# The four stages of an edge network, one group apart or two: a graph-network kernel on one Trainium2 core

## The chip, the core and the metric

The kernel runs on one core of one Trainium2 (trn2) chip. The metric is the device time of one execution in microseconds, without compilation. The median of three runs of the kernel before is 21820.6 us (21802.45 to 21820.88); smaller is better.

Engines are named as in the profile: PE is TensorE's matmul unit and PEld its weight loading, DVE is VectorE, ACT is ScalarE, POOL is GpSimd, SP is SyncE, which here only issues DMAs.

## What is computed

A graph has 6250 nodes with 48 features and 200000 edges sorted by their end node. Four parts follow one another; after each one the result is added to the node features and layer-normed. The second part is the one that matters here:

```python
def _L1_gnn_ref(x, edge_index, edge_feat, W1, b1, W2, b2, W3, b3):
    source, target = edge_index
    edge = jnp.concatenate([x[source], x[target], edge_feat], axis=-1)   # 48 + 48 + 16 = 112
    h = jax.nn.relu(edge @ W1 + b1)                                       # 112 -> 128
    h = jax.nn.relu(h @ W2 + b2)                                          # 128 -> 128
    message = h @ W3 + b3                                                 # 128 -> 48
    msum = jax.ops.segment_sum(message, target, num_segments=n)
    cnt = jax.ops.segment_sum(ones, target, num_segments=n)
    return x + msum / jnp.maximum(cnt, 1.0)[:, None]
...
x = _layernorm(x + _L0_gnn_ref(...)); x = _layernorm(x + _L1_gnn_ref(...))
x = _layernorm(x + _L2_gnn_ref(...)); x = _layernorm(x + _L3_gnn_ref(...))
```

The first part is a four-layer attention over the same edges, the third and fourth are weighted sums of neighbours. All arithmetic of the second part is float32.

## The kernel before

The edges lie as 128 partitions by 1564 columns, so that one column is 128 edges, one in each partition. The columns are worked off in 41 chunks: 38 of 40 columns, then 24, 12 and 8 (`CHUNKS`). Everything is written with a framework that records instructions in program order, lets a scheduler place them on the engines' queues, and adds the semaphore waits. Each engine then works its queue off strictly in that order.

`edge_mlp` is the second part's edge network. For each chunk it does this:

- Two DMAs from SP load `r` (the edges' rows: end nodes, weight, 16 edge features; line 1190) and `q` (the target's features, which stand only in the first edge of each run of equal targets; line 1192).
- `segments_chunk` (lines 801 to 803, DVE) takes from `r` the index `other` of the source node and the mask `ns` of the runs. An ACT copy keeps the edge weight (line 1194).
- POOL gathers the source's features with one indirect DMA for each column (`gather`, line 167): 40 of them for a chunk, into `t[:, j, 0:H]`. The tile `t` has two buffers, so the gathers of chunk c+2 wait until chunk c's `t` has been read.
- `runs` (lines 268, 270 and 287) spreads `q` over each run: ACT copies a quarter of the features to PSUM, DVE adds the value carried from the chunk before and runs a scan over it. ACT then copies the result into `t` (line 1202) and the edge features too (line 1203).
- The network itself works in groups of 4 columns (512 edges), ten groups in a full chunk, in four stages:
  - `turn`: 4 PE transposes into `ps_t` (line 1209), ACT copies them to `at` (line 1211);
  - `first_layer`: one PE product into `ps_1` (line 1216), ACT applies bias and relu into `h1` (line 1218);
  - `second_layer`: one PE product into `ps_1` (line 1223), DVE applies bias and relu into `h2` (line 1225);
  - `third_layer`: 4 PE products into `ps_3` (line 1231), DVE copies them to `msg` (line 1232).
- `runs` sums `msg` over each run (the scans into `sf`), ACT copies the sums to `st` (line 1239) and issues the DMA that stores them.

`ps_t` and `ps_1` have two buffers each, `ps_3` has one; `at`, `h1` and `h2` have the pool's two; `q` has two as well. `skewed` sets the program order of the four stages: in step i the first stage works on group i, the second on group i-1, the third on i-2, the fourth on i-3. So a full chunk has 13 steps, and when the last group is transposed (step 9) the layers of its step and three more steps are left. In the trace a transpose shows as one PE matmul record, the products of lines 1216 and 1223 as two each (float32), the four products of line 1231 as eight, so a group makes 4 + 2 + 2 + 8 = 16 records.

After a chunk's last `msg` copy, ACT and DVE work through the sums of that chunk and the spreading of the next chunk's `q`; only then can the next chunk's transposes begin, since these read `t`, into which line 1202 writes.

Of the kernel before, what the change touches and what calls it, by code (L numbers as in the profile page):

```python
# [9 lines left out]
F32 = mybir.dt.float32  # L10
# [9 lines left out]
P = 128  # L20
N, E, H = 6250, 200000, 48
# [9 lines left out]
HID = 128  # L31
# [5 lines left out]
def pj(t):  # L37
    return t.rearrange("(p j) w -> p j w", j=J)
# [7 lines left out]
def gnn_kernel(ctx: ExitStack, tc: tile.TileContext, A, out: bass.AP):  # L46
# [119 lines left out]
    def gather(dst, table, idx):  # L166
        return nc.gpsimd.indirect_dma_start(  # L167
            out=dst, out_offset=None, in_=table, in_offset=bass.IndirectOffsetOnAxis(ap=idx, axis=0))
# [37 lines left out]
    def by_columns(pool, wid, w, name, cols=C, **kw):  # L206

        return pool.tile([P, cols, w], F32, name=name, **kw)[:, :wid, :]

    def by_features(pool, w, wid, name, cols=C, **kw):  # L210

        t = pool.tile([P, w, cols], F32, name=name, **kw)
        return t.rearrange("p f c -> p (f c)")[:, :w * wid].rearrange("p (f c) -> p f c", c=wid)
# [28 lines left out]
    def factors(pool, name, fg=FG, cols=C):  # L242

        ts = [pool.tile([P, fg, cols], F32, name=f"{name}{i}", bufs=1) for i in range(2)]
        for t in ts:
            V.memset(t, 0.0)

        def put(c, v):
            wid = v.shape[1]
            t = ts[c % 2].rearrange("p f c -> p (f c)")[:, :fg * wid]  # L250
            u = t.rearrange("p (f c) -> p f c", c=wid)
            if wid < cols:
                V.memset(u[:, :, 0:1], 0.0)
            S.copy(u[:, :, 1:], v[:, None, 1:].to_broadcast([P, fg, wid - 1]))
            return t
        return put

    def runs(psum, dst, fac, first, before_, w, put, fg=FG, cols=C):


        wid = dst.shape[2]
        flat = dst.rearrange("p f c -> p (f c)")
        for f0 in range(0, w, fg):
            n = min(fg, w - f0)
            v = by_features(psum, fg, wid, "run_v", cols)
            put(v[:, :n, :], f0, n)
            if before_ is not None:
                V.scalar_tensor_tensor(v[:, :n, 0], before_[:, f0:f0 + n], first, v[:, :n, 0],  # L268
                                       op0=OP.mult, op1=OP.add)
            V.tensor_tensor_scan(flat[:, f0 * wid:(f0 + n) * wid], fac[:, :n * wid],  # L270
                                 v.rearrange("p f c -> p (f c)")[:, :n * wid], 0.0, OP.mult, OP.add)

    def kept_last(pool, t, name):

        k = pool.tile([P, t.shape[1]], F32, name=name)
        V.tensor_copy(k, t[:, :, t.shape[2] - 1])  # L276
        return k
# [4 lines left out]
    def by_column(t):  # L282
        return t.rearrange("p f c -> p c f")

    def copied(src):

        return lambda v, f0, n: S.copy(v, by_feature(src[:, :, f0:f0 + n]))  # L287
# [503 lines left out]
    def segments_begin(k, pool):  # L791
        prev = pool.tile([P, 1], F32, name="seg_prev", bufs=1)
        V.memset(prev, -1.0)
        nc.sync.dma_start(prev[1:P, :], pj(rows[k][:])[0:P - 1, J - 1, 0:1])
        f = pool.tile([P, 1], F32, name="seg_first", bufs=1)
        nc.sync.dma_start(f, pj(rows[k][:])[:, 0, 0:1])
        V.tensor_copy(seg0, f)
        return prev, f

    def segments_chunk(j0, wid, r, prev):  # L800
        V.tensor_copy(other[:, j0:j0 + wid], r[:, :, 1])
        V.tensor_tensor(ns[:, j0:j0 + 1], r[:, 0, 0:1], prev, op=OP.is_equal)
        V.tensor_tensor(ns[:, j0 + 1:j0 + wid], r[:, 1:, 0], r[:, 0:wid - 1, 0], op=OP.is_equal)
        return r[:, wid - 1, 0:1]
# [20 lines left out]
            T.transpose(ps, v.to_broadcast([P, P]), ident)  # L825
            V.tensor_copy(dst, ps)

    def skewed(n, *stages):

        kept = {}  # L830
        for i in range(n + len(stages) - 1):
            for k, stage in enumerate(stages):
                if 0 <= i - k < n:
                    kept[i - k] = stage(i - k, kept.get(i - k))

    carried = const.tile([P, H + 2], F32, name="carried")

# [42 lines left out]
    def first_rows(pool, table, name):  # L880
        t = pool.tile([P, H], F32, name=name, bufs=1)
        gather(t, table[:], seg0[:, 0:1])
        return t
# [6 lines left out]
    def gated_sums(ep, psum):  # L890
# [48 lines left out]
        for c, (c0, wid) in enumerate(CHUNKS):  # L939
# [29 lines left out]
            def outer(i, hi):  # L969
# [5 lines left out]
                V.tensor_mul(by_column(v)[:, j, 0:H], ps.rearrange("p k t w -> p (k t) w"), r[:, j, X0:X0 + H])  # L975

            skewed(-(-wid // 8), turn, hidden, outer)
            for _ in ahead:
                pass
# [201 lines left out]
    def edge_mlp(ep, psum, psum1, psum2):  # L1181
        W = 2 * H + EF
        prev, f = segments_begin("d", ep)
        factor = factors(ep, "fac")
        before_q = first_rows(ep, tab_x, "first")
        before_s = None
        for c, (c0, wid) in enumerate(CHUNKS):
            s = slice(c0, c0 + wid)
            r = by_columns(ep, wid, WD, "r")
            nc.sync.dma_start(r, pj(rows["d"][:])[:, s, :])  # L1190
            q = by_columns(ep, wid, H, "q")
            nc.sync.dma_start(q, pj(spread["d"][0:EP, :])[:, s, :])
            prev = segments_chunk(c0, wid, r, prev)
            S.copy(dw[:, s], r[:, :, 2])
            t = by_columns(ep, wid, W, "t")
            for j in range(wid):
                gather(t[:, j, 0:H], tab_x[:], other[:, c0 + j:c0 + j + 1])
            fac, first = factor(c, ns[:, s]), ns[:, c0:c0 + 1]
            qf = by_features(ep, H, wid, "qf", bufs=1)
            runs(psum2, qf, fac, first, before_q, H, copied(q))  # L1200
            before_q = kept_last(ep, qf, "last_q")
            S.copy(t[:, :, H:2 * H], by_column(qf))
            S.copy(t[:, :, 2 * H:], r[:, :, 3:])
            msg = by_columns(ep, wid, H, "msg", bufs=1)

            def turn(i, _):
                ps = psum.tile([W, 4, P], F32, name="ps_t")
                for k in range(4):
                    T.transpose(ps[:, k, :], t[:, 4 * i + k, :], ident)  # L1209
                at = ep.tile([W, 4, P], F32, name="at")  # L1210
                S.copy(at, ps)  # L1211
                return at

            def first_layer(i, at):
                ps = psum.tile([HID, 4, P], F32, name="ps_1")
                T.matmul(ps, w1, at, start=True, stop=True)  # L1216
                h1 = ep.tile([HID, 4, P], F32, name="h1")
                S.activation(h1, ps, AF.Relu, bias=b1)  # L1218
                return h1

            def second_layer(i, h1):
                ps = psum.tile([HID, 4, P], F32, name="ps_1")
                T.matmul(ps, w2, h1, start=True, stop=True)  # L1223
                h2 = ep.tile([HID, 4, P], F32, name="h2")
                V.tensor_scalar(h2, ps, b2, 0.0, op0=OP.add, op1=OP.max)  # L1225
                return h2

            def third_layer(i, h2):
                ps = psum1.tile([P, 4, H], F32, name="ps_3")
                for k in range(4):  # L1230
                    T.matmul(ps[:, k, :], h2[:, k, :], w3, start=True, stop=True)  # L1231
                V.tensor_copy(msg[:, 4 * i:4 * i + 4, :], ps)

            skewed(wid // 4, turn, first_layer, second_layer, third_layer)
            sf = by_features(ep, H, wid, "sf", bufs=1)
            runs(psum2, sf, fac, first, before_s, H, copied(msg))
            before_s = kept_last(ep, sf, "last_s")
            st = by_columns(ep, wid, H, "st", bufs=1)
            S.copy(st, by_column(sf))  # L1239
            nc.scalar.dma_start(pj(state_h[0:EP, :])[:, s, :], st)  # L1240
        lastf = ep.tile([P, 1], F32, name="lastf", bufs=1)
        V.tensor_copy(lastf, prev)
        return f, lastf, before_s

    with tc.tile_pool(name="e9", bufs=2) as ep:
        with tc.tile_pool(name="e9_ps", bufs=2, space=PSUM) as psum, \
                tc.tile_pool(name="e9_ps1", bufs=1, space=PSUM) as psum1, \
                tc.tile_pool(name="e9_ps2", bufs=2, space=PSUM) as psum2:
            f, lastf, sums = edge_mlp(ep, psum, psum1, psum2)
        with tc.tile_pool(name="e9_ps3", bufs=1, space=PSUM) as psum:  # L1250
            segments_end("d", ep, psum, f, lastf)
            carries(ep, psum, sums, H, 0)
# [112 lines left out]
```

## Time and profile before

| what | value |
|---|---|
| median of the runs | 21820.6 us |
| the profiled execution, its own time | 21803.16 us |
| its span, first to last instruction | 21801.4 us |
| mean granted TensorE clock | 0.621 |
| edge network (lines 1186 to 1240), first gather to last `msg` copy | 14098.9 to 17169.4 us |
| POOL busy over the span | 13861.4 us (64%) |
| PE busy over the span | 5648.7 us (26%) |
| DVE and ACT busy over the span | 8101.9 us (37%) and 4776.3 us (22%) |
| mean duration of one gather, `t<-tab_x` | 1020 ns |

Times are microseconds from the span's start unless marked ns. A timeline line gives start, duration, engine, line, operation, output and inputs, the shape and the count, and in brackets how long the engine had been idle before it and who ended that; "remote" there means that the releaser is not among the instructions the profile can name. A line of the waits gives who waited for whom, the total, the times and the longest wait.

### The profile page before, as it was taken

Reading aid. Unit: us, or ns where it says so; the run is one execution under the profiler, and the core shown is the slowest. Engines: PE = TensorE matmul, PEld = TensorE weight load, DVE = VectorE, ACT = ScalarE, POOL = GpSimd, SP = SyncE. Lnnn points to the kernel's source line nnn. Section 1 sums busy time; section 2 is a strip of 40 time slices with the busy share of each in tenths; the row PEclk is TensorE's granted clock in tenths of the full one; section 3 lists DMA queues with packets and bytes.
Section 4 is the critical chain, followed back from the end, with each engine's and each line's share of the span. In section 5 each row is a group of like instructions: output and inputs, shape, how many; then the busy total and the mean of one; then the engine's idle time right before and its main releaser. Section 6 shows DMA issues by size and latency. Waiting matters only on the chain.

```text
span 21801.4 us, 86436 instructions
## 1 busy us (share of the span) xinstructions
PE 5648.7 (26%) x19138; PEld 3381.8 (16%) x19138; DVE 8101.9 (37%) x16477; ACT 4776.3 (22%) x6603; POOL 13861.4 (64%) x13410
## 2 busy tenths in 40 slices
PE   2332337622222222222222222244544200000000
PEld 2332334410001000110001000133333100000000
DVE  6554557743343434333433343322222211110001
ACT  0332334411111111111111111133333200001111
POOL 2566651177776777677776777644444577777777
PEclk9999995555555555555555555566666655555555
DMA  5455444422222222232222222211111111111111
GB/s 156 160 168 135 163 165 180 168 79 86 85 88 65 88 85 88 65 88 85 88 82 70 86 88 86 59 41 43 43 45 44 34 36 34 36 36 36 36 36 36
DMA packets 873557, 1792.31 MB, mean 82 GB/s; under 512 B 365490, under 2 KB 546658, under 8 KB 868034
## 3 DMA queue, kind: packets, MB, share of 16 engines
q1 hardware_dynamic: 349038, 860.63, 12.1%
q0 software_dynamic: 427520, 547.67, 10.9%
q10 hardware_dynamic: 96468, 378.32, 4.6%
q8 instruction: 163, 2.67, 0.1%
q14 instruction: 368, 3.01, 0.0%
HBM read 1144.48 MB, written 641.17 MB: 82 GB/s over the span
## 4 chain that ended last, share of the span: by engine, by line
POOL 29%; issue 13%; PE 6%; another core or an unknown queue 4%; DVE 3%; ACT 2%; DMA 0%; ACTq 0%; POOLq 0%; DVEq 0%; SPq 0%
POOL t L167 28%; PE ps L1216 2%; PE ps L1223 2%; PE ps L1231 2%; POOL own L167 1%; PE ps_t L1209 1%; ACT run_v L287 1%; ACT st L1239 1%; DVE qf L270 1%; DVE sf L270 1%; DVE run_v L268 0%; DVE q L1134 0%; DMA t<-tab_x,other 0%; ACT at L1211 0%
## 5 line engine op out<-in xcount | busy, mean ns | idle before, releaser
L167 POOL DMA_INDIRECT t<-tab_kv,other x6256 | 6586.8, 1053 | 2117.7 <-issue 2075.2
L167 POOL DMA_INDIRECT t<-tab_x,other x4692 | 4787.2, 1020 | 2619.5 <-issue 1459.6
L1132 PE MATMUL ka<-t,ident 128*128 128x480 f32 (+2 forms) x1264 | 1209.1, 1060 | 6818.1 <-DMA t<-tab_kv,other 5869.4
L172 POOL DMA_INDIRECT rows_s<-r_s,scratch x1564 | 1524.8, 975 | 1032.8 <-ACT r_s L422 528.6
L1134 DVE TENSOR_TENSOR q<-qf,ka 128x480 f32<-128x480 f32 (+2 forms) x632 | 676.6, 1074 | 3791.7 <-issue 3146.9
L1132 PEld LDWEIGHTS ka<-t,ident 128*128 128x128 f32 x1264 | 316.8, 310 | 7533.7 <-issue 4066.5
L270 DVE TENSOR_TENSOR_SCAN qf<-fac,run_v 128x480 f32<-128x480 f32 (+1 forms) x943 | 1028.8, 1092 | 672.1 <-DVE run_v L268 357.1
L841 PE MATMUL cy_ps<-ident,last_s 128*48 128x128 f32 (+1 forms) x4 | 1.6, 405 | 4524.6 <-DVE last_s L276 4524.6
L1164 ACT COPY st<-m 128x40 f32<-128x40 f32 (+3 forms) x164 | 42.8, 261 | 4895.8 <-DVE sc L1137 3754.0
L387 PE MATMUL g<-hs,olt 128*128 128x49 f32 x3128 | 758.7, 417 | 1323.0 <-ACT hs L385 764.4
L287 ACT COPY run_v<-q 128x480 f32<-128x480 f32 (+1 forms) x943 | 851.8, 916 | 707.7 <-DMA q<-spread_s 258.6
L1133 PE MATMUL ka<-r,tenth 128*128 128x400 f32 (+2 forms) x1264 | 954.6, 858 | 0.0
L1225 DVE TENSOR_SCALAR h<-ps,b 128x512 f32<-128x512 f32 x391 | 293.6, 751 | 1710.6 <-PE ps L1216 902.9
L387 PEld LDWEIGHTS g<-hs,olt 128*128 128x128 f32 x3128 | 695.9, 327 | 1375.5 <-ACT hs L385 791.9
L1313 DVE TENSOR_TENSOR run_v<-t,w_ps 128x480 f32<-128x480 f32 (+3 forms) x164 | 142.1, 912 | 1832.9 <-DMA t<-tab_x,other 1832.9
L268 DVE SCALAR_TENSOR_TENSOR run_v<-last_s,ns,run_v 128x12 f32<-128x12 f32 x480 | 98.0, 219 | 1935.4 <-issue 1680.1
L924 POOL TENSOR_TENSOR r<-r,u 128x1920 f32<-128x1920 f32 (+3 forms) x41 | 135.5, 3305 | 1037.0 <-DVE u L923 958.7
L270 DVE TENSOR_TENSOR_SCAN sf<-dec,run_v 128x480 f32<-128x480 f32 (+5 forms) x820 | 731.3, 922 | 122.3 <-remote 57.1
L841 PEld LDWEIGHTS cy_ps<-ident,last_s 128*48 128x48 f32 (+1 forms) x4 | 0.5, 127 | 4525.3 <-ACT st L1319 2261.5
L1216 PE MATMUL ps<-at,w 112*128 112x512 f32 x782 | 535.7, 774 | 496.2 <-ACT h L1218 471.7
L1163 ACT COPY st<-sf 128x1960 f32<-128x1960 f32 (+3 forms) x164 | 621.1, 3787 | 44.9 <-DVE sf L270 25.1
L1156 DVE TENSOR_TENSOR run_v<-t,es 128x480 f32<-128x480 f32 (+2 forms) x656 | 616.7, 962 | 13.9 <-DVE sf L270 5.3
(395 smaller groups left out, 14775.8 us busy)
## 6 DMA issues: line engine op xcount, KB each, us to landing
q<-spread_s SPq DMA_DIRECT2D x190, 960.0 KB
state_a<-st ACTq DMA_DIRECT2D x152, 1000.0 KB
r<-rows_a SPq DMA_DIRECT2D x152, 820.0 KB
state_h<-st ACTq DMA_DIRECT2D x114, 960.0 KB
t<-tab_kv,other POOLq DMA_INDIRECT x6256
r<-rows_s SPq DMA_DIRECT2D x38, 2480.0 KB
t<-tab_x,other POOLq DMA_INDIRECT x4692
seed<-zeros SPq DMA_DIRECT2D x17, 3726.0 KB
```

Of the source, the lines that this page charges most:

```text
L167: return nc.gpsimd.indirect_dma_start(out=dst, out_offset=None, in_=table, in_offset=bass.IndirectOffsetOnAxis(ap=idx, axis=0))
L172: i = nc.gpsimd.indirect_dma_start(out=table, out_offset=bass.IndirectOffsetOnAxis(ap=idx, axis=0), in_=src, in_offset=None)
L270: V.tensor_tensor_scan(flat[:, f0 * wid:(f0 + n) * wid], fac[:, :n * wid], v.rearrange("p f c -> p (f c)")[:, :n * wid], 0.0, OP.mult, OP.add)
L287: return lambda v, f0, n: S.copy(v, by_feature(src[:, :, f0:f0 + n]))
L387: T.matmul(g[:, b0 + b, :], olt[:, b0 + b, :], hs[:, b, :], start=True, stop=True)
L1132: T.matmul(ka, ident, t[:, j0:j1, 0:H], start=True, stop=False)
L1133: T.matmul(ka[:, :, 0:RBF], tenth, r[:, j0:j1, 0:RBF], start=False, stop=True)
L1134: V.tensor_mul(q[:, j0:j1, :], by_column(qf)[:, j0:j1, :], ka)
L1156: V.tensor_mul(v, by_feature(t[:, :, H + 1 + f0:H + 1 + f0 + n]), es[:, None, :].to_broadcast([P, n, wid]))
L1163: S.copy(st[:, :, 0:H + 1], by_column(sf))
L1216: T.matmul(ps, w1, at, start=True, stop=True)
L1223: T.matmul(ps, w2, h1, start=True, stop=True)
```

## The change

The four stages of a group follow one another two groups apart: in step i the first stage works on group i, the second on i-2, the third on i-4, the fourth on i-6. A full chunk has 16 steps instead of 13. The tiles between the stages, `at`, `h1` and `h2`, get three buffers instead of two, and `q` gets one instead of two. No instruction is added or taken away, and the other users of `skewed` keep a distance of one.

```diff
-    def skewed(n, *stages):
+    def skewed(n, *stages, apart=1):
 
         kept = {}
-        for i in range(n + len(stages) - 1):
+        for i in range(n + apart * (len(stages) - 1)):
             for k, stage in enumerate(stages):
-                if 0 <= i - k < n:
-                    kept[i - k] = stage(i - k, kept.get(i - k))
+                g = i - apart * k
+                if 0 <= g < n:
+                    kept[g] = stage(g, kept.get(g))
...
-            q = by_columns(ep, wid, H, "q")
+            q = by_columns(ep, wid, H, "q", bufs=1)
...
-                at = ep.tile([W, 4, P], F32, name="at")
+                at = ep.tile([W, 4, P], F32, name="at", bufs=3)
...
-                h1 = ep.tile([HID, 4, P], F32, name="h1")
+                h1 = ep.tile([HID, 4, P], F32, name="h1", bufs=3)
...
-                h2 = ep.tile([HID, 4, P], F32, name="h2")
+                h2 = ep.tile([HID, 4, P], F32, name="h2", bufs=3)
...
-            skewed(wid // 4, turn, first_layer, second_layer, third_layer)
+            skewed(wid // 4, turn, first_layer, second_layer, third_layer, apart=2)
```

In the built program the order on PE, DVE and ACT differs only inside the edge network; POOL's order is the same, and SP issues the loads of `q` one chunk later.

## The prediction

> **What bounds the kernel now.** The busy shares first, for the even part of the edge network (14200 to 17000 us; the columns are the length, then busy time and count of PE, PEld, DVE, ACT and POOL, then the granted clock, the DMA share and GB/s). No engine is full. So I went on to the waits of the same stretch.
>
> ```profile
> 14200.00:17000.00 2800.00, 1385.54 (x5731) 882.45 (x5732) 793.37 (x1470) 1052.36 (x1185) 1358.99 (x1440) 0.69 0.15 43
> ```
> ```profile
> POOL t L167 <- ACT at L1211: 1006.0, 36, 30.5
> DVE h L1225 <- PE ps L1216: 900.0, 62, 27.7
> ...
> ACT at L1211 <- remote: 413.3, 60, 12.8
> ```
>
> POOL waits 28 us in every chunk until a chunk's last group is transposed and one buffer of `t` is free. ACT and DVE wait long for PE, once a chunk, and no instruction explains it. The timeline of one chunk shows where. I count from its first gather, 15003.71, and call what is left of the older chunk the tail and the next chunk's transposes and what runs beside them the head.
>
> ```profile
> 15002.35 0.61 PE L1209 MATMUL ps_t<-ident,t 128*112 128x128 f32 x4
> ...
> 15003.71 0.94 POOL L167 DMA_INDIRECT t<-tab_x,other  x1 [28.48 <-ACT at L1211]
> ...
> 15010.78 0.36 DVE L1232 COPY msg<-ps 128x192 f32<-128x192 f32 x1 [0.94 <-PE ps L1231]
> 15011.19 1.09 PE L1231 MATMUL ps<-w,h 128*128 128x48 f32 x8 [1.32 <-issue]
> 15015.73 0.36 DVE L1232 COPY msg<-ps 128x192 f32<-128x192 f32 x1 [4.59 <-remote]
> ...
> 15035.38 1.95 PE L1209 MATMUL ps_t<-ident,t 128*112 128x128 f32 x8 [23.09 <-issue]
> 15039.02 1.06 PE L1209 MATMUL ps_t<-ident,t 128*112 128x128 f32 x4
> 15048.82 0.58 ACT L1211 COPY at<-ps_t 112x512 f32<-112x512 f32 x1 [8.87 <-remote]
> 15052.40 0.94 POOL L167 DMA_INDIRECT t<-tab_x,other  x1 [0.30 <-issue]
> 15058.57 0.75 DVE L1225 TENSOR_SCALAR h<-ps,b 128x512 f32<-128x512 f32 x1 [26.95 <-PE ps L1216]
> 15080.55 0.61 PE L1209 MATMUL ps_t<-ident,t 128*112 128x128 f32 x4
> 15081.91 0.94 POOL L167 DMA_INDIRECT t<-tab_x,other  x1 [28.57 <-ACT at L1211]
> ```
>
> The last `msg` copy comes 2 to 4 us after PE shows its product done. Then come 19.65 us of scans (15015.73 to 15035.38). In the head, transposes shown as done at 15040.1 reach ACT only at 15048.82. The gathers end at 15053.3, and from 15058.57 on everything runs evenly to the last transpose. So one period is 49.6 us of gathers plus what is left of the head after them; from 14304.3 to 16943.8 us 34 periods take 77.6 us each.
>
> While POOL gathers, PE's results reach the others late. The price is plainest in the first chunk, which runs wholly beside gathers (they end at 14197.6):
>
> ```profile
> 14141.06 1.78 PE L1231 MATMUL ps<-w,h 128*128 128x48 f32 x8
> ...
> 14149.63 0.58 ACT L1211 COPY at<-ps_t 112x512 f32<-112x512 f32 x1 [16.17 <-remote]
> 14155.18 0.69 ACT L1218 ACTIVATE h<-ps,b 128x512 f32<-128x512 f32 x1 [4.96 <-remote]
> ...
> 14160.79 0.75 DVE L1225 TENSOR_SCALAR h<-ps,b 128x512 f32<-128x512 f32 x1 [21.66 <-remote]
> ...
> 14183.18 0.36 DVE L1232 COPY msg<-ps 128x192 f32<-128x192 f32 x1 [21.64 <-remote]
> ```
>
> These are deliveries in PE's order: 5.55 us for a first product (two records), 5.61 for a second (two), 22.39 for a third (eight). That is 2.8 us for each record, whatever its size. In the steady chunk the limit does not bite at once: of the 42 records that PE still has after a last transpose, 34 are delivered 7.1 us after the first gather and the last one at 12.0. Then PE rests 20 us, ten records of the head pass in time (ACT has the tenth at 15039.26), and the next four take 9.6 us. I read this as an allowance of some 42 records from the first gather on, refilled at one for each 2.8 us: 20 us give seven, and the head's first 4 us more than one, nearly the ten seen. What the mechanism is, the trace does not say. It is over about 4.4 us after the gathers, at +54.
>
> **The change, part by part.** *The order.* In a full chunk of 160 records, the last transpose (step 9) now stands after the first products of groups 0 to 6, the second of 0 to 4 and the third of 0 to 2: 40 + 14 + 10 + 24 = 88 records instead of 40 + 16 + 14 + 48 = 118. After it come 72 instead of 42. Thirty records move from before POOL's release to behind it.
>
> What this gains: the last transpose comes earlier. In the even stretch a step of 16 records takes 2.99 us, in which PE is busy throughout (2.00 of each 2.00 us from 15070 to 15082), so the larger distance makes no step shorter; DVE's 1.81 us waits there cost PE nothing. Thirty records fewer are 30/16 x 2.99 = 5.6 us.
>
> What it costs: the tail. Its first 42 records are delivered by +12, as now. The other 30 come beside gathers at 2.8 us. By +54 that is (54 - 12)/2.8 = 15; the remaining 15 (most of group 8's third product and all of group 9's) go at PE's own speed with the clock at half (1.78 us for eight), with two copies: about 4 us. The last `msg` copy is then at +58, where it is +12 now. Queued behind it in ACT's and DVE's order are this chunk's sums and the next chunk's spreading of `q`, and PE's next transposes wait for these: 19.65 us more, +77.6. The next head then meets no gathers at all. Such a head is in the trace once, behind the 24-column gather run:
>
> ```profile
> 17051.76 1.96 PE L1209 MATMUL ps_t<-ident,t 128*112 128x128 f32 x8 [21.70 <-issue]
> ...
> 17075.32 0.61 PE L1209 MATMUL ps_t<-ident,t 128*112 128x128 f32 x4
> ```
>
> From first to end of last transpose that is 24.2 us; less 5.6 it is 18.6. With 0.75 us to the next gather the period is 58 + 19.65 + 18.6 + 0.75 = 97 us, 19.4 more than now. It happens 36 times (chunks whose successor's successor has 40 columns): +698 us. Behind the 24-column gathers (29.6 us, now 55.3 from gather to gather) the same sum gives 29.6 + 4.4 + 4 + 19.65 + 18.6 + 0.75 = 77: +22. The three short chunks together I put at +10, the first chunk, which reaches its last transpose with fewer slow deliveries, at -10. Sum +720 us.
>
> The bounds: if the tail is through as soon as the limit ends (+54) and the head starts at full clock (its first eight transposes in 1.2 instead of 1.95 us), the period is 54 + 19.65 + 17.9 + 0.75 = 92 (+520 us in all, 22340). If nothing of the 5.6 us is gained in the head, because it begins cold and its first steps wait for ACT's copies, it is 58 + 19.65 + 24.2 + 0.75 = 103 (+900 us, 22720).
>
> *Three buffers for `at`, `h1`, `h2`.* Nothing: they only keep the longer distance from waiting. *One buffer for `q`.* The load of the next `q` is now issued when the current one is read, one chunk before its use instead of two. DMA is busy with it for some 6 us (15028 to 15034), and a period of 77 us or more covers it; without that cover 38 times 6 us, 230 us, would show. On SP's queue the loads of `r` stand between those of `q` and wait for no later event than before.
>
> The profiled execution took 21803.16 us, 17 below the median of the runs, 21820.6. With the sum it would take 22523; stated for the median, 21820.6 + 720, I take 22540 us.
>
> [...]
>
> **The rivals.** *The tail passes beside the gathers* (faster). If the allowance is larger than 72 records, the tail ends 5.6 us later than now, the head begins at +37.3 instead of +31.7, is slow until +54 as now, and has 30 records fewer after that: the period is 72, -5.6 x 37 = -207 us, 21615 us. For it: 34 of 42 records pass now almost unhindered. Against: the last eight come 2 to 4 us late, and the next head has room for just ten. It decides from an allowance of about 63 records (next rival) and is full at 72; the trace says about 42. *The allowance lies between* (no change). With some 60 records the remaining 12 take 34 us, the tail ends near +46, the scans keep the head out of the gathers, and the period is 46 + 19.65 + 19.35 = 85, still slower; only at about 63 records, with the tail ending near +38, do the parts balance at 77.6. A narrow window. *Slower than forecast*: the limit lasts longer than 4.4 us, since PE now has a backlog when the gathers end; 5 us more for each of 37 chunks are 185 us, 22725.
>
> **How the numbers follow.** The forecast with its two bounds and the last rival, slower by over 0.2%: 0.87. The first rival: 0.10. The balance: 0.03. A measurement of this kernel can tell some 0.2% (44 us) from no change. The range from 22260 to 22780 us takes in both bounds (22340 to 22720) and most of the slower rival, and leaves out the faster rival and the far ends.
>
> **What would show it.** Right: POOL's idle time before a gather run grows from 28 to about 47 us; the last `msg` copy of a chunk comes about 58 us after the first gather, behind the gathers' end; ACT's `at` copies in the head no longer wait 8.9 us for "remote"; POOL's mean gather stays near 944 ns. Wrong: `msg` copies that end by +20 while POOL gathers, a period below 77 us, or DVE or ACT waiting for the load of `q`.

## The result and the profile after

The changed kernel takes 22466.77 us (median of four runs, 22428.37 to 22472.21), beside 21813.38 us of the kernel before on the same chip: ratio 1.0302, 95% interval 1.0289 to 1.0315, 653 us slower. Its profiled execution took 22472.21 us and spans 22470.4, 669.0 more than before. The edge network, first gather to last `msg` copy, went from 3070.8 to 3742.7 us (14095.4 to 17838.1): all of the loss lies there. Behind line 828 every line number is one higher than before (1209 is now 1210, 1231 is 1232).

Again the window of the even part first (length, busy time and count of PE, PEld, DVE, ACT and POOL, granted clock, DMA share, GB/s). PE is busy a quarter less in the same 2800 us, the others a fifth less; a gather still takes 946 ns (1097.05/1160).

```profile
14200.00:17000.00 2800.00, 1046.07 (x4662) 713.75 (x4662) 638.76 (x1189) 849.96 (x962) 1097.05 (x1160) 0.65 0.12 35
```

The waits of 14200 to 17600 us (who waited for whom: total, times, longest):

```profile
ACT run_v L287 <- DVE msg L1233: 1754.9, 35, 51.0
POOL t L167 <- ACT at L1212: 1621.5, 36, 47.8
DVE msg L1233 <- remote: 1429.0, 118, 22.1
```

Each is once or a few times a chunk. POOL's wait for a chunk's last transposes is now up to 47.8 us instead of 30.5. The transposes are not at fault: the third line says that DVE's copies wait for something the profile cannot name, and the first that ACT's scans wait for DVE. The timeline of one chunk (first gather 14988.19) shows the order of it, and that what the copies wait for are products which PE's records show as done long before:

```profile
14986.83 0.61 PE L1210 MATMUL ps_t<-ident,t 128*112 128x128 f32 x4
...
14988.19 0.94 POOL L167 DMA_INDIRECT t<-tab_x,other  x1 [46.28 <-ACT at L1212]
...
14996.74 0.36 DVE L1233 COPY msg<-ps 128x192 f32<-128x192 f32 x1 [1.56 <-PE ps L1224]
...
14997.15 1.09 PE L1232 MATMUL ps<-w,h 128*128 128x48 f32 x8 [0.15 <-issue]
...
15005.27 0.36 DVE L1233 COPY msg<-ps 128x192 f32<-128x192 f32 x1 [6.36 <-remote]
...
15019.33 0.36 DVE L1233 COPY msg<-ps 128x192 f32<-128x192 f32 x1 [13.04 <-remote]
...
15019.74 1.94 PE L1232 MATMUL ps<-w,h 128*128 128x48 f32 x8 [12.12 <-issue]
...
15036.96 0.95 POOL L167 DMA_INDIRECT t<-tab_x,other  x1 [0.30 <-issue]
15041.03 0.36 DVE L1233 COPY msg<-ps 128x192 f32<-128x192 f32 x1 [21.34 <-remote]
...
15041.44 1.94 PE L1232 MATMUL ps<-w,h 128*128 128x48 f32 x8 [19.76 <-DVE msg L1233]
15044.58 0.36 DVE L1233 COPY msg<-ps 128x192 f32<-128x192 f32 x1 [3.19 <-PE ps L1232]
...
15044.97 1.86 ACT L287 COPY run_v<-msg 128x480 f32<-128x480 f32 x2 [50.72 <-DVE msg L1233]
...
15064.23 2.88 PE L1210 MATMUL ps_t<-ident,t 128*112 128x128 f32 x12 [20.84 <-ACT t L1203]
...
15084.00 0.95 POOL L167 DMA_INDIRECT t<-tab_x,other  x1 [46.09 <-ACT at L1212]
```

The product that PE begins at 15019.74 and works on for 1.94 us reaches DVE at 15041.03, behind the last gather. (The ends of PE's records are modelled, so the trace does not tell whether PE finishes late or DVE learns of it late; "delivered late" stands for both.) The last `msg` copy begins 56.4 us after the first gather (12.0 before). Scans, head and next gathers follow in a line, so POOL rests from 15037.9 to 15084.0. From 14314.9 to 17558.9 us 34 periods take 95.4 us each (77.6 before).

### The profile page after: what moved, and what is told of

Read it like the earlier page. It is cut to its first block, busy times and chain, and to the rows that moved or that the text cites. A ratio compares the mean times of both kernels' runs of the same rounds, so it can differ in the third digit from the quotient of the medians.

```text
span 22470.4 us, 86512 instructions
## 1 busy us (share of the span) xinstructions
PE 5539.9 (25%) x19138; PEld 3373.3 (15%) x19138; DVE 8094.7 (36%) x16477; ACT 4773.3 (21%) x6603; POOL 13874.5 (62%) x13410
## 4 chain that ended last, share of the span: by engine, by line
POOL 29%; issue 11%; another core or an unknown queue 7%; PE 6%; DVE 4%; ACT 2%; DMA 0%; POOLq 0%; DVEq 0%; SPq 0%; ACTq 0%
POOL t L167 28%; PE ps L1217 2%; PE ps L1224 1%; PE ps L1232 1%; PE ps_t L1210 1%; DVE sf L270 1%; DVE qf L270 1%; POOL own L167 1%; ACT t L1203 1%; ACT st L1240 1%; ACT run_v L287 0%; DVE run_v L268 0%; DVE msg L1233 0%; DVE h L1226 0%
## 5 line engine op out<-in xcount | busy, mean ns | idle before, releaser
L1232 PE MATMUL ps<-w,h 128*128 128x48 f32 x3128 | 502.2, 313 | 1371.3 <-issue 845.7
L1233 DVE COPY msg<-ps 128x192 f32<-128x192 f32 x391 | 139.9, 358 | 1690.9 <-remote 1481.2
L1232 PEld LDWEIGHTS ps<-w,h 128*128 128x128 f32 x3128 | 493.1, 232 | 1534.4 <-issue 998.7
```

## The experiments

In the table "last copy" is the median start of a chunk's last `msg` copy after its first gather, and the period is the mean of 34 chunks of the profiled execution (marked *: 40 gathers of POOL, which does not rest there, and for load_after the mean of four chunks). The ratio is to the kernel before on the same chip, which took 21787 to 21806 us beside the experiments.

| kernel | records behind the last transpose | gather to gather | median us | ratio, 95% interval | period | last copy |
|---|---|---|---|---|---|---|
| before | 42 | 1.25 us | 21813.38 | 1 | 77.6 | +12.1 |
| after | 72 | 1.25 | 22466.77 | 1.0302, 1.0289 to 1.0315 | 95.4 | +56.4 |
| buffers_alone | 42 | 1.25 | 21803.36 | 0.9997, 0.9987 to 1.0006 | 77.8 | +12.1 |
| order_alone | 72 | 1.25 | 22476.37 | 1.0306, 1.0289 to 1.0323 | 95.3 | +56.4 |
| third_58 | 58 | 1.25 | 21787.89 | 1.0001, 0.9991 to 1.0011 | 76.6 | +29.0 |
| third_66 | 66 | 1.25 | 22430.08 | 1.0289, 1.0272 to 1.0306 | 94.1 | +52.8 |
| bf_after | 44 | 1.25 | 21573.12 | 0.9896, 0.9879 to 0.9912 | 71.4 | +15.6 |
| gathers_held | 72, ahead of the gathers | 1.25 | 22086.51 | 1.0131, 1.0114 to 1.0148 | 85.4 | before the gathers |
| paced1_before | 42 | 1.35 | 21698.09 | 0.9965, 0.9951 to 0.9979 | 75.4 | +8.7 |
| paced1_after | 72 | 1.35 | 21677.23 | 0.9950, 0.9934 to 0.9967 | 73.7 | +21.5 |
| paced_before | 42 | 1.57 | 21205.43 | 0.9730, 0.9713 to 0.9746 | 62.8* | beside the next gathers |
| paced_after | 72 | 1.57 | 21210.82 | 0.9728, 0.9712 to 0.9744 | 62.7* | beside the next gathers |
| load_after | 72 | no gathers | 20882.04 | 0.9582, 0.9566 to 0.9598 | 54.6* | |

### The order or the buffers: buffers_alone and order_alone

```diff
 buffers_alone, against the changed kernel
-            skewed(wid // 4, turn, first_layer, second_layer, third_layer, apart=2)
+            skewed(wid // 4, turn, first_layer, second_layer, third_layer, apart=1)
 order_alone, against the changed kernel
-            q = by_columns(ep, wid, H, "q", bufs=1)
+            q = by_columns(ep, wid, H, "q")
```

> Only the buffers of the change (three of at, h1 and h2, one of q), the stages one group apart as before. Theory (records that come behind the last transpose, beside POOL's gathers, are delivered late): still 42 records behind the last transpose, so nothing changes: 21813 us within 0.2%, period 77.6 us, last msg copy at +12. Rival (the single buffer of q, loaded one chunk before its use, or the buffers make the chunk longer): all of the +653 us or a part of it stays, 22000 to 22470 us, and DVE or ACT wait for the load of q.

> The stages two groups apart with three buffers of at, h1 and h2, but q keeps its two buffers. Theory: as the changed kernel, 22467 us within 0.2%, period 95.6 us, last msg copy at +56. Rival (the load of q in its one buffer is what costs): back near 21813 us, less 5.6 us a chunk, 21600 to 21850 us.

The order carries the whole loss. The four buffer changes together are worth nothing in the old order, and the second buffer of `q` is worth nothing in the new one; two buffers of `at`, `h1` and `h2` in the new order were not tried.

### How many records may stand behind the last transpose: third_58 and third_66

In the program order only the fourth stage is moved: five or six groups behind the first instead of three, the others one group apart as before. `h2` has four or five buffers; those of `at`, `h1` and `q` are as in the changed kernel.

```diff
-    def skewed(n, *stages):
+    def skewed(n, *stages, at=(0, 1, 2, 3)):
         kept = {}
-        for i in range(n + len(stages) - 1):
+        for i in range(n + at[len(stages) - 1]):
             for k, stage in enumerate(stages):
-                if 0 <= i - k < n:
-                    kept[i - k] = stage(i - k, kept.get(i - k))
+                g = i - at[k]
+                if 0 <= g < n:
+                    kept[g] = stage(g, kept.get(g))
...
-            skewed(wid // 4, turn, first_layer, second_layer, third_layer)
+            skewed(wid // 4, turn, first_layer, second_layer, third_layer, at=(0, 1, 2, 5))   # third_66: 6
```

> As the kernel before, but the fourth stage (the third layer) five groups behind the first instead of three (h2 with four buffers): 58 records behind the last transpose instead of 42. Theory (a budget of records beside the gathers): by the changed kernel's deliveries (56 of its records out at +31, 64 at +53) the 58th is out at about +37, the scans end at +56, as the limit ends, and a head of 102 records takes 21 us: period 78 us, nearly the 77.6 of before, 21835 us (21750 to 22150). Rival (each record that is moved behind the last transpose costs alike, 18 us for 30): 16 records cost 9.7 us a chunk, 22170 us.

> The same with the fourth stage six groups behind the first (h2 with five buffers): 66 records behind the last transpose. Theory: 64 are out at +53, so the last msg copy is at +54 to +55, the scans and the head come after the gathers: period 95 us, 22450 us (22350 to 22520), a step of over 15 us from eight records more. Rival (each record costs alike): 24 records, 14.5 us a chunk, 22340 us.

Both came as the budget says and not as a price for each record: 16 records more cost nothing (21788 us; at one price for each they would cost 350), and the next eight cost 640. The last copies of one chunk in each, third_58 (first gather 14987.19) and then third_66 (15008.79):

```profile
15004.24 0.36 DVE L1233 COPY msg<-ps 128x192 f32<-128x192 f32 x1 [4.60 <-remote]
...
15016.17 0.36 DVE L1233 COPY msg<-ps 128x192 f32<-128x192 f32 x1 [11.58 <-remote]
```
```profile
15037.81 0.36 DVE L1233 COPY msg<-ps 128x192 f32<-128x192 f32 x1 [11.61 <-remote]
...
15060.21 0.36 DVE L1233 COPY msg<-ps 128x192 f32<-128x192 f32 x1 [22.04 <-remote]
```

The 50th record of third_58 comes at +17. The 58th comes at +29 in both, 8 us sooner than forecast (in 34 of 36 chunks of third_58 between +27 and +40), and the 66th, which only third_66 has there, at +51. With the 58th the 19.65 us of scans still end by +49, and all of it lies beside the gathers, in which the next head could do little anyway. With the 66th they end at +71, 17 us behind the limit's end at about +54, and for these PE stands still.

### Records or time: bf_after

```diff
-                h2 = ep.tile([HID, 4, P], F32, name="h2", bufs=3)
+                h2 = ep.tile([HID, 4, P], BF, name="h2", bufs=3)
...
-                    T.matmul(ps[:, k, :], h2[:, k, :], w3, start=True, stop=True)
+                    T.matmul(ps[:, k, :], h2[:, k, :], w3b, start=True, stop=True)
```

> The changed kernel's order, with h2 and the third layer's weights in bfloat16 (less exact): its four products should show as four records instead of eight, so 44 records stand behind the last transpose instead of 72, in the same instructions. Theory (records count): the tail is through at +12 to +15, the next head begins at +33, some 15 of its 76 records pass by +54, the other 61 take about 17 us: period 72 us, 21600 us (21500 to 21750). Rival (PE's time counts): the third products take half as long, some 0.5 us less a group: 22467 - 36 x 5 = 22290 us.

`w3b` is a bfloat16 copy of `w3`. The third products of a group show as four records (0.26 to 0.32 us together) instead of eight (some 1.0 us):

```profile
14972.25 0.32 PE L1234 MATMUL ps<-w3b,h 128*128 128x48 bf16 x4 [1.86 <-issue]
...
14974.67 0.36 DVE L1235 COPY msg<-ps 128x192 f32<-128x192 f32 x1 [2.48 <-issue]
```

In this chunk (first gather 14959.78) the last copy comes at +14.9; in the median it is +15.6 and the period 71.4, against +12 to +15 and 72 forecast. That the third products got some 0.7 us shorter explains at most 7 of the 24 us that went from each chunk. Against the kernel before a chunk gains 6.2 us, which the shorter products alone could account for; the step from 95.4 to 71.4 they cannot.

### The gathers moved away from the tail: gathers_held

```diff
             skewed(wid // 4, turn, first_layer, second_layer, third_layer, apart=2)
+            held = ep.tile([P, 1], F32, name="held", bufs=1)
+            tc.keep_in_program_order(V.tensor_copy(held, t[:, wid - 1, 0:1]))
```

> The changed kernel with one more DVE copy of a single column of t behind a chunk's last msg copy, so that POOL's gathers into that buffer begin only when the tail is through. The same records in the same order on PE, none of the tail beside gathers. Theory (the gathers make the deliveries late): the tail of 72 records takes 13 to 14 us after the last transpose; counted from the first gather, the scans end and the head begins at +20; 42 of its records pass by about +29, nine more by +54 and some seven from the refill, the remaining 30 take 5.6 us, the last transpose is at about +60, the tail through at +74: period 74 to 75 us, 3 less than the kernel before: 21700 us (21600 to 21850). Rival (the deeper order itself is slow, by PE's clock or by waits among the stages): the tail still takes over 50 us and the gathers now come after it: more than 22467 us, some 23800.

The tail did as forecast: without gathers none of its copies waits over 2.1 us for PE, and the last copy comes 1.3 us ahead of the first gather. So the deeper order is not slow in itself. The time was missed by 390 us, and the fault is in the head. In the chunk whose gathers begin at 14912.07 and its head at 14930.46, eight records pass in time, not 42. The 12th is done at 14933.34 by PE's record and reaches ACT at 14936.79, the 14th comes at 14940.32, and the 18th at 14951.57; from there it goes on as in any other stretch beside gathers:

```profile
14930.46 2.88 PE L1210 MATMUL ps_t<-ident,t 128*112 128x128 f32 x12 [19.68 <-ACT t L1203]
...
14932.46 0.59 ACT L1212 COPY at<-ps_t 112x512 f32<-112x512 f32 x1 [0.27 <-issue]
...
14936.79 0.59 ACT L1212 COPY at<-ps_t 112x512 f32<-112x512 f32 x1 [3.75 <-PE ps L1217]
...
14940.32 0.69 ACT L1219 ACTIVATE h<-ps,b 128x512 f32<-128x512 f32 x1 [2.95 <-remote]
...
14951.57 0.59 ACT L1212 COPY at<-ps_t 112x512 f32<-112x512 f32 x1 [10.56 <-remote]
...
14968.38 0.75 DVE L1226 TENSOR_SCALAR h<-ps,b 128x512 f32<-128x512 f32 x1 [41.59 <-remote]
```

This chunk is one of the slower ones; in the median the 12th record is still nearly in time and the 18th comes 11.8 us after the head's start, where the changed kernel, whose head meets no gathers, has it after 4.6. In the median the last transpose ends at +68 instead of +60, and from there to the next gather it is 17 us instead of 14. So the budget is not a count that a run of gathers hands out whenever PE asks: a run that begins 18 us ahead of PE leaves it some eight to twelve records. The records that PE finished just ahead of the gathers are not what used it up, since in the kernel before 118 of them stand there, and 42 pass all the same. What is left is the gathers themselves, by elimination; no run shows it directly.

### What the gathers have to do with it: the paced kernels and load_after

The paced kernels put a product on an idle tile behind each gather of the edge network, on POOL:

```diff
             for j in range(wid):
-                gather(t[:, j, 0:H], tab_x[:], other[:, c0 + j:c0 + j + 1])
+                tc.keep_in_program_order(gather(t[:, j, 0:H], tab_x[:], other[:, c0 + j:c0 + j + 1]))
+                tc.keep_in_program_order(nc.gpsimd.tensor_mul(pace, pace, pace))
```

`pace` is 128x128 in paced_before and paced_after, 128x1 in the two called paced1.

> The changed kernel with a POOL product of 128x128 values (an idle tile, some 0.3 us) after each gather of the edge network, which stretches a run of gathers from 49.7 to about 62 us. In the changed kernel one chunk alone (first gather at 17002.1) has 1.8 us more between its first two gathers, and there 64 records are out by +21.5 instead of +53. Theory with a budget (a gather takes a little more of something than 1.25 us gives back, and PE's deliveries wait for the rest): slower gathers leave PE free: tail through by +14, next last transpose before the gathers end, period about 63 us set by POOL, 22467 - 36 x 32 = 21300 us. Theory with a fixed limit (one record in 2.8 us as long as POOL gathers at all): the limit lasts until +66, last msg copy at +69, period 108 us, 22467 + 36 x 12 = 22900 us.

> The kernel before with the same POOL product of 128x128 values after each gather of the edge network as in paced_after. Theory (the order matters only through the late deliveries, and these are gone with 1.57 us from gather to gather): POOL sets the time in both, 21211 us within 0.3%. Rival (the change's order has a cost or a gain of its own): more than 0.5% from 21211 us.

More work for POOL made the kernel 2.7% faster. A gather every 1.57 us (two rows of POOL in paced_after, then the last copies of one chunk):

```profile
15003.97 0.42 POOL L1201 TENSOR_TENSOR pace<-pace 128x128 f32<-128x128 f32 x1
15004.55 0.98 POOL L167 DMA_INDIRECT t<-tab_x,other  x1 [0.16 <-issue]
...
15045.90 0.36 DVE L1236 COPY msg<-ps 128x192 f32<-128x192 f32 x1 [1.19 <-PE ps L1235]
...
15047.44 0.36 DVE L1236 COPY msg<-ps 128x192 f32<-128x192 f32 x1 [1.19 <-PE ps L1235]
```

POOL gathers without a rest and the tail passes all the same, at PE's own pace (the last two copies 1.54 us apart); no wait of ACT or DVE in 14200 to 16500 us ends on "remote" (959 us of the `msg` copies' waits do so in the changed kernel in that stretch). Both orders then take the same time, 21205 and 21211 us: with no late deliveries the 17.8 us a chunk of the change are gone. POOL sets the period in both, so a small price of the order would not show here; but load_after, below, runs the changed order at 54.6 us a chunk.

> The kernel before with a POOL product of 128x1 values after each gather of the edge network: by the slope between the 128x128 and the 128x1920 product some 0.2 us, so 1.34 us from gather to gather (1.25 without, 1.57 in paced_before). If PE needs less than 0.09 us between gathers to be free of the limit, POOL sets a period of 54 us: 21205 - 38 x 9 = 20860 us (20800 to 20950). If it needs more, the deliveries stay late in part, over 21205 us, and paced1_after stands above this one by what its tail then costs.

> The same in the changed kernel. Limit gone: as paced1_before, 20860 us. Limit there in part: the tail of 72 records is caught and this one is slower than paced1_before.

The gathers came 1.35 us apart, where 1.34 was forecast, and there the limit is in force in part: of the `msg` copies' waits in 14200 to 16500 us 191 us end on "remote", beside 959 in the changed kernel. The tail of 72 records is out at +21.5, so the kernel does much what the first rival of the prediction described, an allowance that the tail fits into: its period is 73.7 us, the rival had 72. (That the two numbers are so close is partly luck, since the run of gathers is 4 us longer here and the limit weaker.) The expected loss of the changed order against the other did not come; the two intervals overlap.

```diff
-            for j in range(wid):
-                gather(t[:, j, 0:H], tab_x[:], other[:, c0 + j:c0 + j + 1])
+            nc.sync.dma_start(t[:, :, 0:H], pj(spread["d"][0:EP, :])[:, s, :])
```

> The changed kernel, but t is filled by one DMA from SP for each chunk (the same bytes, contiguous rows of the spread table instead of the rows of the sources, so the messages are others); POOL issues no gathers in the edge network. Theory (POOL's gathers make PE's deliveries late): nothing is late; tail 13.5 + scans 19.65 + head 18.6 + under 1 us: period 52 to 53 us, 22467 - 36 x 43 = 20900 us (20800 to 21000). Rival (the rows that are written into t make them late, whoever asks for them): the tail still comes late by several records while the load runs, period over 58 us, over 21150 us.

As expected, 20882 us. Over 14200 to 15800 us DMA moves more than in the changed kernel (62 GB/s against 34, in 161788 packets against 28661), and behind a load issued at 15002.25 the tail's last copy comes at 15017.23, and no copy of that tail waits over 1.2 us for PE. What makes PE's results late is POOL's gathers at 1.25 us each, not the bytes or packets that arrive in `t`.

### On another chip: paced64_before

`pace` is 128x64 here, in the order of before.

> The kernel before with a POOL product of 128x64 values after each gather of the edge network, between the two sizes tried: about 1.44 us from gather to gather. If that is enough to free PE, POOL sets a period of some 57.7 us: 21205 - 38 x 5 = 21010 us (20960 to 21080), the fastest so far with the whole computation. If the limit still bites in part, as at 1.34 us, the next head is caught and the time lies above 21205 us.

This comparison ran on a chip on which the kernel before takes 18664.62 us (18663.4 to 18667.7), 3100 less than on the three other chips of these experiments. The paced kernel takes 18879.15 us there, ratio 1.0115 (1.0099 to 1.0132): slower. A gather begins every 1.46 us, POOL gathers without a rest, a period is 58.5 us, and no wait in 12500 to 14600 us, within the edge network, ends on "remote". The attention part, which no edit touches, is quicker there too. Its gathers in paced_before and then in paced64_before (busy time, mean ns, idle time before them):

```profile
L167 POOL DMA_INDIRECT t<-tab_kv,other x6256 | 6561.0, 1049 | 2139.4 <-issue 2110.3 <-DMA t<-tab_kv,other 16.4 <-DVE q L1134 12.7
```
```profile
L167 POOL DMA_INDIRECT t<-tab_kv,other x6256 | 5903.0, 944 | 1906.5 <-issue 1862.0 <-DVE q L1134 32.6 <-DMA t<-tab_kv,other 11.9
```

From the difference of the medians, 214.5 us over 38 chunks, the kernel before has a period of about 53 us there (an estimate; no profile of it on that chip exists). That is close to the 54.6 us that load_after needs with nothing late, so the limit seems to be absent there, and the pauses only cost. Whether 1.46 us would be enough on the other chips, and what the change does on this one, was not tried.

## Why the prediction was right

*What stands behind the last transpose decides.* Right. Moving 30 records there cost 17.8 us in each chunk; order_alone has all of it, buffers_alone none. The zero for the one buffer of `q` was right too; that three buffers of `at`, `h1` and `h2` only keep the longer distance from waiting was not tested.

*The tail.* The forecast was 42 records by +12, 15 more by +54, the last 15 within 4 us. Measured in the chunk above: 36 by +8.5, 48 by +17, 56 by +31, 64 by +53, the last eight at +56.4. The budget is nearer 50 than 42, the records after it come at first quicker than one in 2.8 us (eight in 14 us, then eight in 22), and so eight are left for the end instead of 15. The copy came 1.6 us earlier than forecast. That a budget too low by eight cost so little is partly luck: some records are left over when the gathers end in either case, and the gathers' end sets the end of the tail.

*Scans, head, period.* The scans add 19.6 us (56.4 to 76.0), and from there to the next gather it is 19.7 us in the median, against 18.6 + 0.75. The 5.6 us that the shorter head should gain are there but for 0.4. The median period is 95.75 against 97, the 1.6 us of the tail less these 0.4; the mean is 95.4 because one chunk of the 34 takes only 77.5 (the last section has it).

*The sum.* From the third chunk's gathers at 14219.1, the first that wait for a tail, to the 24-column ones at 17654.4, 36 intervals cost 641 us more than before (forecast 698). The 24 columns cost 77.1 - 55.3 = 21.8 (22), the first chunk gained 4.7 (10), and what is left of the 672 us, 14, falls on the short chunks (10). The term that was too large is the 36 chunks' 19.4 us each: 17.8 were measured, 1.25 less by the median chunk and the rest by that one chunk.

*The rivals.* The first, that the tail passes beside the gathers, needed an allowance of 63 records to balance, nine fewer than the tail has, and 72 for its gain. With a budget of some 50 the kernels with 58 and 66 records, eight and sixteen over it, lie on both sides of these nine: no loss and 2.9%. The course that it describes occurs with the gathers at 1.35 us. The balance did not occur with 72 records, and the limit did not outlast the gathers: after the last gather's end at 15037.9 the next delivery comes at 15041.03.

*What was read wrongly.* The prediction called the budget an allowance "from the first gather on". The chunks of gathers_held, with eight to twelve records in time after 18 us of gathers without PE, say by elimination that gathers alone use it up too. For the change itself it made no difference, since its tail begins with the gathers; for gathers_held it was worth 390 us.

## What to carry to other kernels

When one engine's last step of a stage releases another engine's long run, everything that still stands behind that step runs beside the run: count it in the unit that the run makes scarce, here PE's records and not PE's microseconds (44 records left the last copy at +15.6, 72 at +56.4), before a pipeline is made deeper. Such a cost can come as a step, here nothing at 58 records and 2.9% at 66, so one size that costs nothing says little about the next. And where an engine's results arrive late while it is idle, try slowing down the engine beside it: a pause of 0.3 us behind each gather was worth 2.7%, while on another chip a gather every 1.46 us cost 1.2%.

## What the runs showed of the hardware

- PE's results beside POOL's indirect gathers depend on how closely the gathers follow one another: at 1.25 us about 50 records pass from a run's start and then, after a slower stretch, one comes in some 2.8 us (eight in 21.7 us in the changed kernel, in 22.4 in third_66); at 1.35 us, in paced1_after, 72 pass by +21.5; at 1.57 us, in paced_after, all are in time. On these chips the lateness ends somewhere between the last two.
- One chunk shows it without any edit of the gathers. In the changed kernel the gathers of the chunk at 17002.10 have a gap of 2.10 us once, between the first two, and its last `msg` copies come at 17023.64 and 17039.08, at +21.5 and +37 instead of +53 and +56. Its period is then 77.5 us, what a chunk took before:

```profile
17005.13 0.94 POOL L167 DMA_INDIRECT t<-tab_x,other  x1 [2.10 <-issue]
...
17023.64 0.36 DVE L1233 COPY msg<-ps 128x192 f32<-128x192 f32 x1 [6.72 <-remote]
...
17039.08 0.36 DVE L1233 COPY msg<-ps 128x192 f32<-128x192 f32 x1 [15.08 <-remote]
```

  The same gap stands between the first two gathers of the same chunk in every kernel with gathers 1.25 us apart, and in each whose tail runs beside them that tail is early: the last copy comes at +8.7 instead of +12.1 in the kernel before, at +14.5 instead of +29.0 in third_58, at +24.4 instead of +52.8 in third_66, at +32.8 instead of +56.4 in order_alone. Why the gap is there, the traces do not say.

- On three chips the kernel before takes 21787 to 21806 us, on a fourth 18664.62. That nothing is late on the fourth is an estimate, from its period of about 53 us beside the 54.6 of load_after. What differs there, and what PE's results and the gathers share on the others, stays open; the runs show only that the rate of the gathers and the number of PE's records decide. Every run on record comes with the profiler's span and clock, so it is open too whether recording the instructions has a part in it.
